# Two graph-attention layers on one Trainium2 core: edge weights in three operations, another order of the stages, one pool for the large arrays

## The chip, the cores and the metric

The kernel runs on one core of one Trainium2 chip. The core has TensorE (PE) for matrix products, VectorE (DVE), ScalarE (ACT) and GpSimd (POOL) for the rest, and SyncE (SP), which here issues most of the DMA transfers. Each engine takes its instructions in the order in which the program wrote them, and waits for the others by semaphores. The metric is the device time of one execution in microseconds, as the median of several runs. Lower is better.

## The reference

The input is a batch of 32 graphs of 512 nodes with 512 features (x, float32) and their adjacency (32 x 512 x 512 integers). Two layers follow, each on a normalised and rectified copy of x, and each added to x:

```python
h = jnp.maximum(_layernorm(x, axis=-1), 0.0)
x = x + _L0_gnn_ref(h, adj, ...)      # one head, no projection
h = jnp.maximum(_layernorm(x, axis=-1), 0.0)
x = x + _L1_gnn_ref(adj, h, ...)      # 512 -> 4 heads of 256, ELU, then 1024 -> 512 with one head
```

All three attentions (layer 0, and the two inside layer 1) have the same form. Every node has two scores, a and c, which are dot products of its features with two vectors. The weight between two nodes is the softmax of a leaky ReLU (slope 0.2) of a + c, taken over the neighbours only:

```python
e = jax.nn.leaky_relu(asrc[:, :, None, :] + adst[:, None, :, :], NEG_SLOPE)
e = jnp.where(mask[..., None], e, NEG_INF)
attn = jax.nn.softmax(e, axis=1)
out = jnp.einsum('bsdh,bshf->bdhf', attn, xl)
```

## The kernel before

**Tiles.** The 512 nodes of a graph are T = 4 blocks of 128 partitions (P). A matrix of weights E is a tile of 128 x 4 x 512 float32: block t of the rows, all 512 columns. A graph has six of them: one for layer 0, four for the heads of layer 1's first attention, one for its second.

**Stages of a graph.** `layer0_scores` (normalise, rectify, two dot products a block on DVE, the masks, the edge weights), `layer0_out` (E times h, added to x), `layer1_in` (normalise, rectify, transpose h on PE, spill x to DRAM), `layer1_project` (the product with W1, by a scheme of seven products of half-size blocks in place of eight, `products`), `layer1_scores` and `layer1_head` for each of four heads, `layer2_project`, `load_back` (x from DRAM) and `layer2_out`. The product with W also gives the scores a and c, as two more columns. All products are float32; PE shows two records for each. The attention products are at L688 (`aggregate`), those with W at L904 (`product`).

**The edge weights** (`edge_weights`, L638 to 679). The score a is made a row (512 values, the same on all partitions) in a PSUM bank. DVE adds the mask to it and takes the maximum (L647, four times), so that every column n has the largest neighbouring a; from that and c comes the guard m, the largest exponent of each column (L653, L655). The guard is made a row, too. Then each of the four blocks takes four operations: ACT computes the leaky ReLU of row c plus column a (Prelu, L669), DVE subtracts the guard's row (L672), POOL adds the mask, which is 0 or a large negative number (L675), and ACT takes the exponential (L678). The division by the sum comes after the product, by a column of ones that stands beside the values (L700, L974).

**Two ways to make a row of a column.** `spread` (L585) transposes the column, broadcast to 128 x 128, on PE: four transposes (L510) into one PSUM bank. `in_lines` (L603) transposes the narrow columns once (L609), copies them out of PSUM, and writes them to a small DRAM array, `lines` (L615); `row_of` (L620) reads a line back to all 128 partitions (L625), into one of three buffers `row`; `in_bank` (L632) copies such a row to PSUM by ACT (L635). The scores of layer 1's heads go through `lines`. The guards of layer 0 and of the second attention go through `lines` as well, except in the first and the last graph. The guards of layer 1's four heads go through `spread`, by the last argument of the call in `layer1_scores`, `edge_weights(ac(0), ac, lines, 2 * j, m1T, m1, True)`.

**Masks.** POOL's queue loads the adjacency of a graph (L729) twice, for layer 0 and for layer 1, and SP issues its transpose (L739).

**The order of the work.** The kernel records each operation with its engine, an assumed cost, its dependences and the buffers that it takes, and a planner (`Plan`) orders them all before anything is emitted. It runs through time: whichever engine is free next takes the ready operation with the lowest rank. A buffer is taken when the first operation that needs it is placed and is free after the last; kinds named in `in_turn` are handed out in the order of the program. The rank is the position in the program, less a share of the operation's `ahead` (400 for rows and first constants, -300 for what is needed later). Six shares are tried, each with a second draft ranked by the latest start that the first draft allows (`latest`), and the draft with the earliest end is emitted. The loop over graphs b (L1091 on) has this order: masks and projection of b; read-back and output of b-1; load of x(b+2); the four heads of b, each with its weights one head ahead; layer 0's output and layer 1's input of b+1; layer 0's scores of b+2; second projection and weights of b.

**Buffers.** x 2, masks 5 in four kinds, h 1, hT 1, pair 3, xl2 1, E 5, row 3, spill 2, eight PSUM banks (acc).

## Time and profile before

| | |
|---|---|
| median of 3 runs | 3626.27 us |
| fastest and slowest run | 3624.45 and 3626.67 us |
| profiled execution, its own time as the profile gives it (its span) | 3621.9 us |
| busy: PE, DVE, ACT, POOL | 3537.2, 2814.5, 2214.8, 1500.5 us |
| moved by DMA | 378.82 MB |
| row reads from `lines` | 442 of 256 KB, 3.3 us from issue to landing |

The profiled execution has no time but the span, from its first to its last instruction; the median of the runs is 4.4 us more. How to read the lines: in the table of engines stand the busy microseconds, the share of the span and the number of instructions. The slices cut the span in 40 and give busy tenths. The chain that ended last goes back from the last instruction to what released it, and so on; its shares say which engine and which line the end hangs on. A row of a timeline has start, duration, engine, line, operation, output and inputs, and in brackets the idle time before it and what ended that. Durations of PE overlap, so the cost of one of its instructions is the distance of two starts.

### The profile page before, as it was taken

The page shows a single profiled execution, that of the slowest core. Times are in us where ns is not written, and L with a number is a line of the kernel's source. Part 1 is how long each engine was busy: PE and PEld are TensorE (multiplying, and loading weights), DVE is VectorE, ACT ScalarE, POOL GpSimd, SP SyncE. Part 2 cuts the span into 40 slices and gives each one's busy share as a digit, 9 for nine tenths or more (in the row PEclk, how much of TensorE's full clock was granted, in tenths as well). Part 3 has the DMA queues.
Part 4 walks back from the last instruction along what each step waited for, and adds up shares of the span by engine and source line. Part 5 has one row for each costly group of instructions (what it writes and reads, how often), then busy time and mean ns, then how long its engine had stood idle before and what let it go on. Part 6 is the DMA issues. An engine that isn't in the chain of part 4 may idle for free.

```text
span 3621.9 us, 50432 instructions
## 1 busy us (share of the span) xinstructions
PE 3537.2 (98%) x16852; PEld 3039.8 (84%) x16852; DVE 2814.5 (78%) x7468; ACT 2214.8 (61%) x3801; POOL 1500.5 (41%) x1306
## 2 busy tenths in 40 slices
PE   4899999999999999999999999999999999999998
PEld 3788888888888888888888888888888888888887
DVE  7978778777778787778787788777787877787755
ACT  2665566665666665666655666655666656666554
POOL 4534335443344343344344354443443433453432
PEclk9999999999999999999999999999999999999999
DMA  6254333444334443334443334443344433344321
GB/s 171 56 126 116 91 97 107 105 123 105 99 96 111 110 120 97 100 104 102 122 114 96 98 107 101 124 113 91 99 112 105 120 98 100 104 105 117 103 75 43
DMA packets 510375, 378.82 MB, mean 105 GB/s; under 512 B 348345, under 2 KB 386977, under 8 KB 510113
## 3 DMA queue, kind: packets, MB, share of 16 engines
q1 hardware_dynamic: 476320, 342.03, 33.0%
q0 software_dynamic: 33792, 33.56, 6.5%
q8 instruction: 132, 2.16, 0.2%
q14 instruction: 131, 1.07, 0.1%
HBM read 257.16 MB, written 68.01 MB: 90 GB/s over the span
## 4 chain that ended last, share of the span: by engine, by line
PE 88%; DVE 2%; DMA 1%; issue 0%; POOL 0%; ACT 0%; DVEq 0%; SPq 0%; ACTq 0%
PE acc L688 44%; PE acc L904 39%; PE acc L510 4%; DVE junk L647 1%; PE acc L609 1%; DVE E L672 0%; POOL E L675 0%; DMA lines<-row 0%; DMA row<-lines 0%; DVE x L706 0%; DVE v L977 0%; ACT acc L635 0%; ACT E L669 0%; DVE col L655 0%; DVE col L653 0%
## 5 line engine op out<-in xcount | busy, mean ns | idle before, releaser
L675 POOL TENSOR_TENSOR E<-E,m 128x512 f32<-128x512 f32 x640 | 759.4, 1215 | 545.8 <-DVE E L672 413.7
L688 PE MATMUL acc<-pair,E 128*128 128x257 f32 (+1 forms) x4160 | 935.0, 380 | 5.9 <-ACT E L678 3.9
L688 PEld LDWEIGHTS acc<-pair,E 128*128 128x128 f32 x4160 | 783.0, 189 | 122.0 <-ACT E L678 4.7
L678 ACT ACTIVATE E<-E 128x512 f32<-128x512 f32 x768 | 472.9, 623 | 218.1 <-POOL E L675 217.1
L904 PE MATMUL acc<-w_T,E 128*128 128x257 f32 (+1 forms) x2048 | 515.7, 380 | 0.2 <-POOL w_T L492 0.2
L669 ACT ACTIVATE E<-row,ac 128x512 f32<-128x512 f32 x760 | 507.5, 710 | 3.2 <-DMA row<-lines 3.0
L672 DVE TENSOR_TENSOR E<-E,acc 128x512 f32<-128x512 f32 x768 | 491.7, 675 | 19.0 <-ACT acc L635 11.7
L688 PE MATMUL acc<-h,E 128*128 128x257 f32 (+1 forms) x2048 | 487.0, 382 | 16.3 <-ACT E L678 16.3
L688 PE MATMUL acc<-xl,E 128*128 128x257 f32 x1984 | 448.9, 380 | 2.7 <-ACT E L678 2.7
L647 DVE CUSTOM_DVE_ANT_0 junk<-m1T,acc 128x512 bf16<-128x512 bf16 x640 | 436.0, 681 | 15.0 <-PE acc L510 3.4
L688 PEld LDWEIGHTS acc<-h,E 128*128 128x128 f32 x2048 | 385.0, 191 | 70.8 <-ACT E L678 17.5
L904 PEld LDWEIGHTS acc<-w_T,E 128*128 128x128 f32 x2048 | 385.3, 190 | 56.3 <-POOL w_T L492 0.6
L688 PEld LDWEIGHTS acc<-xl,E 128*128 128x128 f32 x1984 | 371.2, 190 | 53.3 <-ACT E L678 2.9
L917 DVE TENSOR_TENSOR pair<-acc,pair 128x258 f32<-128x258 f32 (+1 forms) x390 | 165.0, 424 | 320.3 <-PE acc L904 258.5
L543 ACT COPY pair<-acc 128x258 f32<-128x258 f32 (+1 forms) x400 | 147.6, 370 | 297.3 <-PE acc L904 293.5
L729 POOL DMA_DIRECT2D m<-in_adj_dram x64 | 51.6, 806 | 590.9 <-DVE col L647 540.7
L533 ACT ACTIVATE h<-x,col,col 128x512 f32<-128x512 f32 x256 | 187.6, 804 | 176.4 <-issue 108.8
L675 POOL TENSOR_TENSOR E<-E,m0T 128x512 f32<-128x512 f32 x128 | 144.7, 1155 | 353.5 <-DVE E L672 353.5
L543 ACT COPY xl<-acc 128x257 f32<-128x257 f32 x190 | 68.8, 369 | 331.3 <-PE acc L904 331.3
L904 PE MATMUL acc<-w,hT 128*128 128x258 f32 x1024 | 269.6, 383 | 0.0
L904 PE MATMUL acc<-w,E 128*128 128x257 f32 (+1 forms) x1024 | 267.7, 381 | 0.0
L977 DVE SCALAR_TENSOR_TENSOR v<-acc,r,b_r 128x256 f32<-128x256 f32 x512 | 244.5, 478 | 9.2
(108 smaller groups left out, 5524.3 us busy)
## 6 DMA issues: line engine op xcount, KB each, us to landing
row<-lines SPq DMA_DIRECT2D x442, 256.0 KB, 3.3
x<-in_x_dram SPq DMA_DIRECT2D x32, 1024.0 KB, 13.6
m<-in_adj_dram POOLq DMA_DIRECT2D x64, 512.0 KB, 5.7
spill<-x SPq DMA_DIRECT2D x32, 1024.0 KB, 4.4
x<-spill SPq DMA_DIRECT2D x32, 1024.0 KB
out_dram<-x SPq DMA_DIRECT2D x30, 1024.0 KB, 4.2
v<-row SPq DMA_TRANSPOSE x192, 2.7
out_dram<-x SPq DMA_DIRECT2D x8, 256.0 KB, 2.0
```

The source lines that it names most:

```text
L510: op("PE", on_pe(P, transpose=True), lambda: nc.tensor.transpose(dst_of(), src_of(), identity), src, dst(part), ahead)
L533: lambda: nc.scalar.activation(h.at[:, t, :D], X.at[:, t, :], AF.Relu, bias=nmr.at[:, t : t + 1], scale=rstd.at[:, t : t + 1]),
L543: nc.scalar.copy(dst_of(), src_of())
L647: lambda t=t: nc.vector.tensor_tensor_reduce(by_blocks(junk), mask_row(mask_max, t), by_blocks(a_row.at), 1.0, LOWEST, ALU.add, ALU.max, a ...
L669: lambda t=t: nc.scalar.activation(E.at[:, t, :], c_row.at, AF.Prelu, bias=a_of(t), scale=1.0, alpha=SLOPE),
L672: op("DVE", on_dve(N), lambda t=t: nc.vector.tensor_sub(E.at[:, t, :], E.at[:, t, :], m_row.at), m_row(*ROW) + E(t), E(t))
L675: lambda t=t: nc.gpsimd.tensor_add(by_blocks(E.at[:, t, :]), by_blocks(E.at[:, t, :]), mask_row(mask, t)),
L678: op("ACT", on_act(N), lambda t=t: nc.scalar.activation(E.at[:, t, :], E.at[:, t, :], AF.Exp), E(t), E(t))
L688: lambda s=s: nc.tensor.matmul(acc.at[:, :n], E.at[:, s, node_block(t)], of(s), start=(s == 0), stop=(s == T - 1)),
L904: lambda k=k: nc.tensor.matmul(acc.at[:, :width], at[a]()[:, k, node_block(r)], weight_of(w, k, c), start=(first and k == 0), stop=(k == n ...
L917: op("DVE", on_dve(width), lambda: nc.vector.tensor_add(place(), acc.at[:, :width], place()), acc(0) + token, token)
L977: lambda i=i, v=v, acc=acc, r=r: nc.vector.scalar_tensor_tensor(v.at[:, i, :], acc.at[:, :F], r.at, b1_r[:, h * F : (h + 1) * F], op0=ALU. ...
```

## The change

- **Edge weights.** Since leaky(a + c) is a + 0.2 c + max(0.8 c, -0.8 a), and 0.2 c is the same for a whole column of the softmax, the weights are computed as exp(a + max(0.8 c, -0.8 a) + mask - g), where g is the guard less 0.2 c. The vectors that give c are scaled by 0.8 once (`scaled`). A block takes three operations: POOL subtracts g's row from the mask, DVE takes the maximum of row c (in PSUM) and a column and adds POOL's result, ACT takes the exponential with column a as bias.
- **Guards.** They have a function of their own (`guards`), for both heads of a pair at once. All go through `lines`, but for the first graph's layer 0 and the last graph's second attention. The rows of g and c are read into the last two blocks of the tile E itself.
- **Order.** `layer2_project` of b-1 comes after the projection of b; two heads' weights come first, then layer 0's output and layer 1's input of b+1, the load of x(b+2), the heads, layer 0's scores, and the read-back and output of b-1 last.
- **Leads.** The position in the program is replaced by the PE work ahead of the operation, less a lead for its stage (`LEADS`, a table in microseconds; a star stands for PE's operations, "first" and "last" for the first and last graphs). One draft is made.
- **Pools.** h, hT, pair, xl2 and E share eleven places (`big`), handed out in any order; the masks share five in turn; `row` has two places, spill four.

```diff
-    AHEAD, DRAFTS = (0.25, 0.5, 0.75, 1.0, 1.25, 1.5), 1
+    LEADS = {
+        "first LXsoon": -3, "first Csoon": -892.2, "first C": -652.8, "first Clater": -1055, "first S0": -896.9,
+        "first S0M0": -82.9, "first S0g": 0, "first S0g*": 1.5, "first S0e*": -109.4, "first S0e": -112.3,
+        "first O0*": -186.7, "first O0": -606.7, "first I1": 109.2, "first I1*": 57.3, "first LX": -57.3,
+        "first S0*": 51.5, "M1": -176.1, "P1": 226.4, "P1*": -47.2, "S1": -178.5, "S1*": 2390.8, "S1g": 0.2,
+        "S1g*": 11.1, "S1e": -430.4, "O0*": -17, "O0": -41.5, "I1": 243.9, "I1*": 1.2, "LX": 103.4, "H*": -14.8,
+        "H": 677, "S0": -969.2, "S0M0": 0.1, "S0*": -7.8, "S0g": 0, "S0g*": 2.2, "S0e": -22, "P2": 297.1, "P2*": 3.6,
+        "P2g": 183, "P2g*": 72.1, "P2e": -385.7, "LB": 167.8, "O2*": -83.3, "O2": -311.4, "last M1": 12.4,
+        "last P1": -359.3, "last P1*": 175.2, "last P2": -440.7, "last P2*": 163.9, "last P2g": 201.5,
+        "last P2g*": 165.4, "last P2e": -174.1, "last S1": -53.8, "last S1*": 674.7, "last S1g": -338.7,
+        "last S1g*": 107.8, "last S1e": 93.3, "last H*": 160.8, "last H": -242.6, "last LB": -4, "last P2e*": 130.2,
+        "last O2*": -97.7, "last O2": -248.8,
+    }
...
+        rank, work, best = [], 0.0, None
+        for engines, cost, _, _, _, lead, _ in self.ops:
+            rank.append(work - 1e3 * self.LEADS[lead])
+            if engines[0] == "PE":
+                work += cost[0][0]
...
-        "m0": places("m0", 1, [P, T, N], BF16),
-        "m0T": places("m0T", 1, [P, T, N], BF16),
-        "m1": places("m1", 2, [P, T, N], BF16),
-        "m1T": places("m1T", 1, [P, T, N], BF16),
-        "h": places("h", 1, [P, T, D + 1]),
-        "hT": places("hT", 1, [P, KD, N]),
-        "pair": places("pair", 3, [P, T * 2 * XL]),
-        "xl2": places("xl2", 1, [P, T, 2 + D + 1]),
-        "E": places("E", 5, [P, T, N]),
+        "m": places("m", 5, [P, T, N], BF16),
+        "big": places("big", 11, [P, T * 2 * XL]),
...
-    plan = Plan(slots, ("x", "spill", "m0", "m0T", "m1", "m1T", "h", "hT", "pair", "xl2", "v"))
+    plan = Plan(slots, ("x", "spill", "v", "m"))
...
+        scaled(lambda: ws_r, D, W["w0"](0), W["w0"]("src"), SOON)
+        scaled(lambda: b0_r, 1, W["w0"](2), W["w0"]("rest"), SOON)
+        scaled(lambda: flat(att[0])[:, HF : 2 * HF], HF, att[0](1), att[0](1), LATER)
...
+    @plan.part("g")
+    def guards(scores, ac, lines, n, mask_max, near):
+        op(
+            "DVE", on_dve(n * T), lambda: nc.vector.tensor_scalar(ac.at[:, 4 : 4 + n, :], ac.at[:, 0 : 2 * n : 2, :], SLOPE - 1.0, None, op0=ALU.mult),
+            scores, ac("negated"),
+        )
+        g = Buffer("guard")
+        for j in range(n):
+            a_of = lambda t, j=j: ac.at[:, 2 * j, t : t + 1]
+            a_row = spread(scores, a_of) if near & 1 else in_bank(row_of(lines, 2 * j))
...
+        if near & 2:
+            return g, None
+        return g, in_lines(lambda: g.at[:, :n, :].rearrange("p n t -> p (n t)"), g(*range(n)), n)
...
+    @plan.part("e")
+    def edge_weights(scores, ac, lines, j, guard, mask):
+        g, guard_lines = guard
+        E = Buffer("big", as_rows)
+        c_at, g_at = (lambda: E.at[:, T - 2, :]), (lambda: E.at[:, T - 1, :])
+        if guard_lines is None:
+            bank = spread(g(j) + E("place"), lambda t: g.at[:, j, t : t + 1])
+            op("ACT", on_act(N), lambda: nc.scalar.copy(g_at(), bank.at), bank(*ROW), E(T - 1))
+        else:
+            row_of(guard_lines, j, g_at, E(T - 1))
+        c_of = lambda t: ac.at[:, 2 * j + 1, t : t + 1]
+        c_row = spread(scores + E("place"), c_of) if lines is None else in_bank(row_of(lines, 2 * j + 1, c_at, E(T - 2)))
         for t in range(T):
             op(
+                "POOL", on_pool(N, True),
+                lambda t=t: nc.gpsimd.tensor_sub(by_blocks(E.at[:, t, :]), mask_row(mask, t), by_blocks(g_at())),
+                E(T - 1) + mask(*ROW), E(t), lock=True,
+            )
+            op(
+                "DVE", on_dve(N, 1.0, True),
+                lambda t=t: nc.vector.scalar_tensor_tensor(
+                    E.at[:, t, :], c_row.at, ac.at[:, 4 + j, t : t + 1], E.at[:, t, :], op0=ALU.max, op1=ALU.add
                 ),
+                c_row(*ROW) + E(t) + ac("negated"), E(t),
+            )
...
-            op("DVE", on_dve(N), lambda t=t: nc.vector.tensor_sub(E.at[:, t, :], E.at[:, t, :], m_row.at), m_row(*ROW) + E(t), E(t))
...
-            op("ACT", on_act(N), lambda t=t: nc.scalar.activation(E.at[:, t, :], E.at[:, t, :], AF.Exp), E(t), E(t))
...
+                lambda t=t: nc.scalar.activation(E.at[:, t, :], E.at[:, t, :], AF.Exp, bias=ac.at[:, 2 * j, t : t + 1]),
...
+        plan.stage = "last " if b == B - 1 else ""
         masks1(b)
         layer1_project(b)
         if b:
-            load_back(b - 1)
-            layer2_out(b - 1, ROW if b < B - 1 else ROW[:EARLY], b < B - 1)
-        if b + 2 < B:
-            load_x(b + 2)
-        Es = []
-        for h in range(H):
-            Es.append(layer1_scores(b, h))
-            if h:
-                layer1_head(b, h - 1, Es[h - 1])
-        layer1_head(b, H - 1, Es[H - 1])
+            layer2_project(b - 1)
+        Es = [layer1_scores(b, 0), layer1_scores(b, 1)]
         if b + 1 < B:
             layer0_out(b + 1)
             layer1_in(b + 1)
         if b + 2 < B:
+            load_x(b + 2)
+        for h in range(H):
+            if h + 2 < H:
+                Es.append(layer1_scores(b, h + 2))
+            layer1_head(b, h, Es[h])
+        if b + 2 < B:
             layer0_scores(b + 2)
-        layer2_project(b)
-
+        if b:
+            load_back(b - 1)
+            layer2_out(b - 1, ROW if b < B - 1 else ROW[:EARLY], b < B - 1)
+    layer2_project(B - 1)
     layer2_out(B - 2, ROW[EARLY:], False)
     load_back(B - 1)
     layer2_out(B - 1, ROW, False)
```

## The prediction

> **What bounds the kernel now.** I read the engine table and the slices first, to see which engine is full and where it is not, then the chain that ended last, then PE's waits by stage, and last PE's own timeline in one graph, to price what the change takes from it.
>
> ```profile
> span 3621.9 us, 50432 instructions
> PE 3537.2 (98%) x16852; PEld 3039.8 (84%) x16852; DVE 2814.5 (78%) x7468; ACT 2214.8 (61%) x3801; POOL 1500.5 (41%) x1306
> PE   4899999999999999999999999999999999999998
> ...
> PE 88%; DVE 2%; DMA 1%; issue 0%; POOL 0%; ACT 0%; DVEq 0%; SPq 0%; ACTq 0%
> PE acc L688 44%; PE acc L904 39%; PE acc L510 4%; DVE junk L647 1%; PE acc L609 1%; DVE E L672 0%; POOL E L675 0%; DMA lines<-row 0%; DMA row<-lines 0%; DVE x L706 0%; DVE v L977 0%; ACT acc L635 0%; ACT E L669 0%; DVE col L655 0%; DVE col L653 0%
> ```
>
> PE is full and carries the chain; nothing else has over 2%. L688 are the attention products, L904 the projections, L510 the transposes in sets. The stages (columns: length; busy us and instructions by engine; granted clock; DMA share; GB/s) say where PE still stands:
>
> ```profile
> 0.00:100.00 100.00, 47.05 (x185) 37.85 (x186) 75.77 (x230) 24.75 (x46) 40.56 (x40) 0.93 0.60 157
> 100.00:200.00 100.00, 87.31 (x397) 71.55 (x397) 84.07 (x219) 58.33 (x96) 46.04 (x40) 0.97 0.27 76
> 400.00:1000.00 600.00, 599.78 (x2872) 516.92 (x2871) 468.86 (x1246) 373.46 (x652) 246.84 (x218) 1.00 0.42 108
> 3500.00:3622.00 122.00, 106.58 (x474) 89.28 (x473) 69.05 (x170) 59.60 (x102) 34.25 (x29) 0.92 0.18 55
> ```
>
> From 400 to 3500 us PE stands still for 1.8 us in all (3100 less the four stages' 599.78, 999.83, 998.70, 499.92). There only PE's own work counts. All else it loses is at the two ends: 53 us in the first 100, 13 in the next, 15 in the last 122.
>
> **PE's work: the guards' transposes.** Before, every head of layer 1 turns its guard column into a row with four transposes on PE (`spread`, called with near true). After, one transpose for two heads, a write to DRAM and two broadcast reads do it. 32 graphs x 4 heads = 128 sets of four go, 64 single ones come: 448 PE instructions fewer of 16852. A window of PE's timeline inside one graph (start, duration, line):
>
> ```profile
> 1005.44 0.65 PE L510 MATMUL acc<-ident,col 128*128 128x128 f32 x4
> 1005.92 3.63 PE L688 MATMUL acc<-xl,E 128*128 128x257 f32 x16
> ...
> 1014.78 0.65 PE L510 MATMUL acc<-ident,col 128*128 128x128 f32 x4
> 1015.27 8.84 PE L688 MATMUL acc<-pair,E 128*128 128x257 f32 x40
> ...
> 1023.95 0.60 PE L510 MATMUL acc<-ident,col 128*128 128x128 f32 x4
> 1024.38 1.89 PE L688 MATMUL acc<-h,E 128*128 128x257 f32 x8
> ...
> 1084.55 0.27 PE L609 MATMUL acc<-ident,col 128*4 128x128 f32 x1
> 1084.66 0.60 PE L904 MATMUL acc<-w,E 128*128 128x258 f32 x2
> ```
>
> The durations overlap, so I count from start to start: a set costs 0.48, 0.49 and 0.43 us, mean 0.467; a single one 0.11. 128 x 0.467 - 64 x 0.11 = 59.7 - 7.0 = **52.7 us less** (48.0 at 0.43, 55.7 at 0.49). All matmuls stay: 240 a graph, two records each. Since PE is covered by nothing in those 3100 us, this comes off the end in full if the rest keeps up.
>
> **The edge weights: three operations a tile in place of four.** Gone: ACT's Prelu (760 + 8, 512 us busy) and DVE's subtraction (768 x 675). New: POOL subtracts the guard row from the mask (same shapes as the addition that it replaces, 1155 to 1215 ns), DVE does max and add with the score row in PSUM, ACT does Exp with a bias column (taken as the Prelu with its column, 512 us in place of 473). The DVE form is not in the trace at 512 columns. Bounds: 675, as the subtraction that reads PSUM; 834, as L998's two-tensor form at 512 in SBUF. L977 and L706, the same instruction with PSUM at 256, take 477; adding 256 columns at (675 - 424) / 254 = 0.99 ns (L672 against L917) gives 730, which I take: +42 us on DVE in all. The sum for DVE, with 128 small multiplications of a score column (L802's kind, 224 ns: 29), is 2885 us, 81% of the new span. ACT: -512, +39 for the bias, +111 for 190 score rows copied to PSUM (585 each), -36 for 62 guard rows no longer copied, +16 for 64 evictions (254): 1833 us. None of this is on the path in the long stage: PE hides it, and by 20 us a graph (DVE 86 of 109.7 us). If that cover were gone, DVE's +0.07 us would count on each tile.
>
> **The guards' rows.** 128 more row reads (338 ns of SP issue each: 43 us) and 64 more line writes (304 ns: 19 us), 33.5 MB more on 378.8; the DMA engines are 42% busy. The latency of a guard grows from 1.1 us (four transposes) to transpose 0.3, eviction 0.25, write 1.8, read 3.3: 5.7 us, and the read now lands in the tile E itself, so that SP waits for a free place and all rows, mask transposes and spills behind it wait too. The nearest row is the identical round trip of the scores, already there 64 times in layer 1: it is inside the 1.8 us of waits. Bounds: 0, as those; upwards 2.7 to 2.8 us (PE's wait for Exp in the first and last graphs) on each of 64 pairs, 175 us. I take 5 us, since the near row says almost nothing.
>
> The Trainium skill's "DMA: Bandwidth & Descriptors", section "Latency and other measured facts", speaks against this part: about 2 us of fixed cost for every DMA, most of it the round trip to HBM. Two trips would be 4 us by it, against the 5.1 us of this trace; by either the guard is late unless the order has it 4 to 6 us early.
>
> **Order and pools.** The second layer's projection of graph b moves behind the first layer's of b+1 (56 products, 24 us at 0.434); its output moves to the end of that turn; two heads' weights come ahead of the next graph's output of layer 0. Moved with them: the line writes and row reads and the read-back of x on SP (now behind the load of graph b+2), and the masks' loads on POOL, which already waits 591 us in all ahead of them. Five mask places are still five, eleven large ones still eleven (1+1+3+1+5), only handed out freely. On average this costs nothing: the cover is PE's backlog; without it a late x is 13.6 us, once a graph. The leads replace six trial orders by one order; a lead says how far ahead or behind its place in PE's work an operation ranks.
>
> **Start.** Now PE's first product waits until 44.10 us: SP issues the transposed mask only at 30.54, behind the weights, POOL starts on it at 42.06, although the guards are there at 29.96. After, by the leads, SP takes x(0), x(1), ten transfers of layer 1's vectors and weights, and only then ws_r. Now those eight weight loads are issued until 14.8; so ws_r would be issued at about 16 and land (its row: 5.7) at 22, against dots that now start at 11.42. Then 6.0 us of dots, 0.7 of transposes, 3.0 of maxima, 0.3, four transposes 1.1, a copy 0.6, POOL 1.2, DVE 0.7, ACT 0.7: 36 to 38 us. The mask's transpose ranks ahead of the last nine loads: issued at 20 to 26, plus the present 11.5, 32 to 38. I take the start at 40: **-4**. Bounds: -13 (the mask issued as soon as it is made, at 19) and +10 (dots delayed in full on top of the present order).
>
> **End.** Now the last graph's edge weights stand uncovered:
>
> ```profile
> 3597.19 1.11 PE L510 MATMUL acc<-ident,col 128*128 128x128 f32 x4 [3.01 <-DVE col L655]
> 3601.05 16.99 PE L688 MATMUL acc<-pair,E 128*128 128x257 f32 x64 [2.74 <-ACT E L678]
> ```
>
> From PE's last projection (it would end about 3592.1) to 3601.05 are 9 us, of which 1.1 is transposes, and the last 64 products take 17.0 us where 64 x 0.217 is 13.9. After, output of graph 30 (64 records, 14 us) ranks behind the last projection (leads -97.7 against +163.9) and can stand in that gap. Filled, 8 + 3 = 11 us go; unfilled, the new chain is 0.6 us longer (a copy). I take **-7**. The granted clock is 0.92 in this stage.
>
> The skill's "TensorE: Matmul & The Clock Gate", section "What's actually happening", says that an idle window of 3.4 us halves the clock until one busy window has passed; that loses 1.7 us, an estimate, where the row loses 3.1. By it the end would give 9.8 in place of 11.
>
> **Sum.** -52.7 + 5 - 4 - 7 = -58.7 us. The profiled execution's span is 3621.9, which would become 3563.2; the median of the runs, 3626.27, lies 4.4 us above it, and I carry that over: **3567.6, say 3568**. A measurement of this kernel tells about 0.2%, 7 us.
>
> **Rivals.** (1) The start gains in full as well: 12 in place of 4 there, 11 at the end, no new stalls: 3626.3 - 52.7 - 23 = 3551. For it: separate leads for the first and last graphs. Against: ws_r so late in SP's queue. (2) The gain is partly given back: heads wait for guards on a third of the 64 pairs by 1 to 1.5 us (some 20 to 32 us), no gain at the ends: 3626 - 53 + 26, about 3599. For it: margins are thin now (one tile of weights finishes at 1032.5 and the 32 records of a head start at 1035.2); against: 1.8 us of waits. (3) Slower: SP holds the guard's row back. Now six transposes of v, which wait for ACT, stretch over 20.35 us of SP's queue from 1019.94; a row read behind them is up to 20 us late, and every later row behind a read that waits for E's place. It decides from 64 pairs x 0.92 us = 59 us; at 2 us a pair the time is 3626 - 59 + 128 = 3695. Against: the rows of the scores stand in the same queue now and cost nothing. (4) The planner's new order does not do what it says and PE's idle grows as much as its work falls: 3626.
>
> **How the numbers follow.** Forecast (3556 to 3582): 0.53. Rival 1 (3540 to 3556): 0.16. Rival 2 (3582 to 3619): 0.15. Rival 4 (within 7 us): 0.04. Rival 3: 0.12. Faster 0.84, same 0.04, slower 0.12. Outside 3543 to 3620 lie rivals 3 and 4 and a fifth of rival 1, some 0.19. The cost of DVE's new form at its ends (-42, +80 us from the one taken, off the path) moves none of it while PE covers it.
>
> **What would show it.** PE with 448 fewer instructions and L510's sets for col gone but for the first and last graphs; PE's waits from 400 to 3450 us under 10 us; ACT near 1830, DVE near 2890; the first product near 40 us; no wait of 8 us ahead of the last 64 products. Wrong it is if PE waits for Exp or for a guard's eviction once in every graph.

## The result, and the profile after

| | before | after |
|---|---|---|
| median of the runs | 3624.79 us | 3635.08 us |
| fastest and slowest run | 3623.02 and 3626.67 | 3627.05 and 3642.64 |
| span of the profiled execution | 3621.9 us | 3636.5 us |

The ratio is 1.0025, with an interval of 1.0019 to 1.0032: a little slower, where 1.6% faster was forecast. The page of the kernel after: its span, its table of engines, PE's slices, and the chain that ended last, by engine and by line:

```profile
span 3636.5 us, 49863 instructions
PE 3487.2 (96%) x16404; PEld 2998.4 (82%) x16404; DVE 2834.7 (78%) x7596; ACT 1891.2 (52%) x3204; POOL 1500.9 (41%) x1394
PE   3999999999999999999999999999999999999999
...
PE 76%; DVE 10%; DMA 9%; issue 2%; POOL 1%; ACT 0%; SPq 0%; POOLq 0%; DVEq 0%
PE acc L988 37%; PE acc L760 36%; DMA m<-in_adj_dram 8%; DVE junk L698 3%; PE acc L553 2%; DVE big L741 2%; PE acc L652 1%; DMA big<-lines 1%; DVE x L778 1%; DVE col L705 1%; DVE guard L710 1%; DVE st L559 1%; POOL big L736 1%; DVE v L1086 1%; DVE m L855 1%
```

PE has the 448 instructions fewer and 50.0 us less work. But the chain no longer stays on PE: 88% have become 76%, and a load of the adjacency (`m<-in_adj_dram`), which isn't among the lines of the chain before, holds 8%. In the new numbering the attention products are L760, the projections L988, the transposes L553, a single narrow transpose L652. The table by stage (length; busy us and instructions of PE, PEld, DVE, ACT, POOL; clock; DMA share; GB/s):

```profile
0.00:100.00 100.00, 39.34 (x149) 30.76 (x150) 77.96 (x227) 20.81 (x32) 39.93 (x40) 0.91 0.66 168
100.00:400.00 300.00, 291.79 (x1368) 247.99 (x1367) 257.49 (x705) 175.37 (x298) 135.74 (x122) 0.99 0.42 106
400.00:3500.00 3100.00, 3025.91 (x14280) 2607.70 (x14279) 2416.92 (x6476) 1639.18 (x2789) 1283.33 (x1197) 1.00 0.44 114
3500.00:3637.00 137.00, 130.15 (x613) 111.96 (x611) 82.31 (x189) 55.80 (x86) 41.91 (x35) 1.00 0.23 68
```

A stage's length less PE's busy time is PE's idle time. The whole difference of the two profiled executions comes out of it:

| | before | after | difference |
|---|---|---|---|
| PE busy | 3537.2 | 3487.2 | -50.0 |
| PE idle, 0 to 400 us | 67.6 | 68.9 | +1.2 |
| PE idle, 400 to 3500 us | 1.8 | 74.1 | **+72.3** |
| PE idle, from 3500 us to the end of the span | 15.3 | 6.4 | -9.0 |
| sum, the span | 3621.9 | 3636.5 | +14.6 |

So the gain was made, and given back in the steady graphs. PE's waits of the kernel after in that stretch (total us, times, longest us) are two, each once in a graph:

```profile
PE acc L760 <- DVE v L1065: 45.3, 27, 3.9
PE acc L652 <- DVE guard L710: 28.7, 27, 2.1
```

DVE itself waits in the same stretch for the adjacency:

```profile
DVE m L855 <- DMA m<-in_adj_dram: 56.1, 27, 4.3
```

**The first wait: the mask.** `v L1065` is an eviction on DVE that takes half a microsecond and depends on nothing new. A timeline of one graph (start, duration, engine, line, operation, in brackets the idle time before it and what ended that; SPq is SP issuing a transfer) shows what stands ahead of it:

```profile
1013.36 0.37 SPq L922 DMA_DIRECT2D spill<-x  x1
1014.36 0.37 SPq L791 DMA_DIRECT2D x<-in_x_dram  x1
1018.48 0.36 SPq L931 DMA_DIRECT2D x<-spill  x1
1018.70 0.82 POOL L802 DMA_DIRECT2D m<-in_adj_dram  x1 [0.30 <-DVE r L1062]
...
1030.13 0.69 DVE L855 TENSOR_SCALAR m<-m 128x2048 bf16<-128x2048 bf16 x1 [2.95 <-DMA m<-in_adj_dram]
1032.20 0.48 DVE L1065 SCALAR_TENSOR_TENSOR v<-acc,r,b_r 128x256 f32<-128x256 f32 x1
...
1032.73 3.08 PE L760 MATMUL acc<-big,big 128*128 128x257 f32 x8 [2.54 <-DVE v L1065]
```

POOL issues the adjacency's load 0.2 us after SP has issued the third of three 1 MB transfers. It lands 11.4 us later. DVE has the first operation on the mask (L855) as its next instruction, stands 2.95 us for it, and the eviction that would free a PSUM bank waits behind it. Then PE stands. The kernel before had the same four transfers, but far apart:

```profile
996.48 0.79 POOL L729 DMA_DIRECT2D m<-in_adj_dram  x1 [0.30 <-POOL E L675]
...
1005.30 0.68 DVE L777 TENSOR_SCALAR m<-m 128x2048 bf16<-128x2048 bf16 x1
...
1014.49 0.39 SPq L718 DMA_DIRECT2D x<-in_x_dram  x1
...
1059.71 0.36 SPq L840 DMA_DIRECT2D spill<-x  x1
...
1063.94 0.36 SPq L848 DMA_DIRECT2D x<-spill  x1
```

There the adjacency landed after 5.7 us, and the same mask operation (then L777, at 1005.30, 9 us after the load's issue) never waited. A graph loads its adjacency twice, and only layer 1's load, the one shown, is late now: over the 27 steady graphs it lands after 10.4 us (median; 9.5 to 12.7) in place of 5.7, while layer 0's lands after 5.5. (The page's medians over all 64 loads, 5.7 and 6.9, mix the two.) The new order of the stages brought the four transfers together.

**The second wait: a guard.** It is the guard of the second attention, which went through `lines` before the change too. PE's narrow transpose stands 0.79 us for it in this graph:

```profile
984.73 18.13 POOL L736 TENSOR_TENSOR big<-m,big 128x512 f32<-128x512 bf16 x16 [19.55 <-DMA big<-lines]
...
1000.88 0.76 DVE L705 TENSOR_TENSOR col<-ac,col 128x4 f32<-128x4 f32 x1
...
1001.96 0.92 DVE L710 SCALAR_TENSOR_TENSOR guard<-col,col 128x4 f32<-128x4 f32 x1
...
1003.02 0.27 PE L652 MATMUL acc<-ident,guard 128*4 128x128 f32 x1 [0.79 <-DVE guard L710]
```

Two operations on 128 x 4 elements take 0.76 and 0.92 us, while POOL works through sixteen subtractions of the edge weights in a row. When POOL is idle they take 0.16. Counted over 400 to 3400 us, for single operations of DVE (mean us, number), by whether POOL was at work on arrays at their start (POOL's issue of a transfer is counted as idle):

| kernel, line, operation | reads | POOL at work | POOL idle |
|---|---|---|---|
| before, L525, `col<-mv,col` 128x4 | two tensors in SBUF | 1.227 (28) | 0.163 (27) |
| before, L653, `col<-ac,col` 128x4 | two in SBUF | 0.513 (27) | 0.149 (137) |
| before, L655, `col<-col` 128x4 | two in SBUF (the same twice) | (0) | 0.148 (164) |
| after, L705, `col<-ac,col` 128x4 | two in SBUF | 0.982 (54) | 0.158 (108) |
| after, L710, `guard<-col,col` 128x4 | two in SBUF | 0.910 (27) | 0.154 (135) |
| after, L560, `mv<-st` 128x2 | one in SBUF | 0.176 (86) | 0.172 (130) |
| after, L687, `ac<-ac` 128x4 and 128x8, times a constant | one in SBUF | 0.951 (33) | 0.167 (75) |
| after, L741, `big<-acc,ac,big` 128x512 | one in PSUM, one in SBUF | 0.739 (486) | 0.736 (162) |

The kernel before has the same effect, as two of its rows show (POOL at work until 802.85):

```profile
797.68 5.17 POOL L675 TENSOR_TENSOR E<-E,m 128x512 f32<-128x512 f32 x4 [5.57 <-DVE E L672]
...
800.97 0.72 DVE L653 TENSOR_TENSOR col<-ac,col 128x4 f32<-128x4 f32 x1
```

But its guard operations met POOL 27 times, and L655 never; in the kernel after the two that replace them meet it 81 times.

### The profile page after: what moved, and what is told of

Same layout as the page of the kernel before. It is cut to its first block, busy times and chain, and to the rows that moved or that the text cites. A ratio compares the mean times of both kernels' runs of the same rounds, so it can differ in the third digit from the quotient of the medians.

```text
span 3636.5 us, 49863 instructions
## 1 busy us (share of the span) xinstructions
PE 3487.2 (96%) x16404; PEld 2998.4 (82%) x16404; DVE 2834.7 (78%) x7596; ACT 1891.2 (52%) x3204; POOL 1500.9 (41%) x1394
## 4 chain that ended last, share of the span: by engine, by line
PE 76%; DVE 10%; DMA 9%; issue 2%; POOL 1%; ACT 0%; SPq 0%; POOLq 0%; DVEq 0%
PE acc L988 37%; PE acc L760 36%; DMA m<-in_adj_dram 8%; DVE junk L698 3%; PE acc L553 2%; DVE big L741 2%; PE acc L652 1%; DMA big<-lines 1%; DVE x L778 1%; DVE col L705 1%; DVE guard L710 1%; DVE st L559 1%; POOL big L736 1%; DVE v L1086 1%; DVE m L855 1%
## 5 line engine op out<-in xcount | busy, mean ns | idle before, releaser
L760 PE MATMUL acc<-big,big 128*128 128x257 f32 (+1 forms) x8192 | 1876.2, 381 | 61.7 <-DVE v L1065 47.8
L760 PEld LDWEIGHTS acc<-big,big 128*128 128x128 f32 x8192 | 1540.8, 190 | 307.1 <-DVE v L1065 59.9
L736 POOL TENSOR_TENSOR big<-m,big 128x512 f32<-128x512 bf16 x768 | 889.6, 1186 | 667.6 <-DMA big<-lines 455.9
L988 PE MATMUL acc<-w_T,big 128*128 128x258 f32 (+1 forms) x3072 | 776.4, 382 | 1.6 <-DVE big L968 1.6
L988 PE MATMUL acc<-w,big 128*128 128x258 f32 (+1 forms) x3072 | 769.2, 381 | 0.9 <-POOL big L969 0.6
L748 ACT ACTIVATE big<-big,ac 128x512 f32<-128x512 f32 x768 | 539.9, 719 | 265.6 <-DVE big L741 258.0
L988 PEld LDWEIGHTS acc<-w_T,big 128*128 128x128 f32 x3072 | 582.4, 191 | 91.3 <-DVE big L968 2.0
L988 PEld LDWEIGHTS acc<-w,big 128*128 128x128 f32 x3072 | 572.1, 190 | 87.1 <-ACT big L586 1.0
L741 DVE SCALAR_TENSOR_TENSOR big<-acc,ac,big 128x512 f32<-128x512 f32 x768 | 555.6, 738 | 23.7 <-POOL big L736 20.7
L698 DVE CUSTOM_DVE_ANT_0 junk<-m,acc 128x512 bf16<-128x512 bf16 x768 | 525.1, 684 | 18.5 <-DVE ac L687 0.4
L988 PE MATMUL acc<-w_-T,big 128*128 128x258 f32 (+1 forms) x1024 | 254.3, 380 | 1.9 <-DVE big L1001 1.9
L1065 DVE SCALAR_TENSOR_TENSOR v<-acc,r,b_r 128x256 f32<-128x256 f32 x512 | 246.0, 481 | 7.4
L988 PEld LDWEIGHTS acc<-w_-T,big 128*128 128x128 f32 x1024 | 191.5, 189 | 33.7 <-DVE big L1001 3.4
L576 ACT ACTIVATE big<-x,col,col 128x512 f32<-128x512 f32 x256 | 195.7, 804 | 23.2 <-DVE col L568 20.4
```

The lines of the kernel that those rows point to most:

```text
L698: lambda t=t, amax=amax, a_row=a_row: nc.vector.tensor_tensor_reduce(by_blocks(junk), mask_row(mask_max, t), by_blocks(a_row.at), 1.0, LOW ...
L736: lambda t=t: nc.gpsimd.tensor_sub(by_blocks(E.at[:, t, :]), mask_row(mask, t), by_blocks(g_at())),
L741: lambda t=t: nc.vector.scalar_tensor_tensor(E.at[:, t, :], c_row.at, ac.at[:, 4 + j, t : t + 1], E.at[:, t, :], op0=ALU.max, op1=ALU.add),
L748: lambda t=t: nc.scalar.activation(E.at[:, t, :], E.at[:, t, :], AF.Exp, bias=ac.at[:, 2 * j, t : t + 1]),
L760: lambda s=s: nc.tensor.matmul(acc.at[:, :n], E.at[:, s, node_block(t)], of(s), start=(s == 0), stop=(s == T - 1)),
L988: lambda k=k: nc.tensor.matmul(acc.at[:, :width], at[a]()[:, k, node_block(r)], weight_of(w, k, c), start=(first and k == 0), stop=(k == n ...
```

## The experiments

Two theories for the standing time were to be told apart from each other and from the prediction's own rivals. (A) The adjacency is late because of the transfers beside it, and DVE, which works in order, passes the delay to PE. (B) The second attention's guard is late because POOL holds back DVE's small operations. The rivals: the rows of layer 1's guards through DRAM cost the time after all; or DVE is simply behind, so that each wait that is removed comes back elsewhere. In the diffs, `plan.shift` holds one operation back, with what depends on it, in the emitted order, behind the given number of operations of its own engine; the rest of the order stays.

**1. The mask's operations later.**

```diff
-        load_adj(b, m1)
+        load_adj(b, m1); plan.shift += [(len(plan.ops) + n, 12) for n in range(1 + T) if b > 2]
```

> The changed kernel with one thing moved: from the fourth graph on, DVE's five operations that make layer 1's mask out of the loaded adjacency stand some twelve DVE operations later; all other orders are the same. Theory: DVE waits there for an adjacency transfer that lands later than the planner assumed (56 us from 400 to 3500 us), and through it PE waits for the eviction behind (45 us, and a lower clock after each wait). Then PE's waits for v go and the time falls from 3635 by 45 to 65 us, to 3570 to 3590. Rival: PE has run out of prepared weights and waits at the next late step instead; then the time stays above 3620.

Measured: 3591.4 us (3589.5 to 3593.7), a ratio of 0.991 (0.9895 to 0.9924) to the kernel before. The wait for v is gone from the steady graphs; one of 13.7 us (27 times) for layer 0's scores has come, and the guard's is still there with 24.8. Most of theory A's gain appears, 1.4 us short of the expected range.

**2. The guard's transpose later.** The second attention's transpose of its guard stands six products later on PE.

```diff
-        if near & 2:
-            return g, None
+        if near & 2: return g, None
+        plan.shift += [(len(plan.ops), 6)] if plan.stage == "P2g" else []
```

> The changed kernel with one thing moved: PE's single transpose of the second attention's guard stands six products (2.6 us) later, with what hangs on it. Theory: PE waits about 1 us a graph (28.7 us from 400 to 3500) because DVE's two small operations for the guard take 0.8 and 0.9 us in place of 0.15 while POOL works beside them. Then this wait goes: 3635 - 29 = 3606, 3598 to 3612. Rival: the wait for v grows by what is gained here, or POOL's weights come late by 2.6 us a graph; then 3630 or more.

Measured: 3639.5 us (3636.7 to 3644.9), ratio 1.0044 (1.0029 to 1.0059): no gain. PE's waits:

```profile
PE acc L760 <- DVE v L1065: 49.0, 27, 4.1
PE acc L553 <- ACT big L576: 7.4, 28, 0.3
PE acc L760 <- DVE x L778: 6.2, 13, 1.1
```

The guard's wait is gone, but 17 of its 28.7 us stand at the other three now, and the time shows nothing of the rest. While DVE loses 2.2 us a graph to the mask (60.0 us in 27 waits of L855 in this run), a later transpose hides little. The expected time was missed.

**3. Both.**

> Both moves at once. Theory: all steady waits of PE go, 74 us of standing and 5 to 20 us of lowered clock: 3541 to 3561, about 3553, which is the sum that was forecast without the stalls. Rival (the pools or the longer guard chain are short in themselves): other waits come in, above 3600.

Measured: 3588.7 us (3586.2 to 3589.5), ratio 0.9901 (0.9884 to 0.9917). Not the sum: 2.7 us better than the mask's operations alone, far above the expected 3541 to 3561, and below the rival's 3600 too. 11.2 us for layer 0's scores, 6.7 for an ACT operation and 5.5 for the eviction of x remain: some of what is held back is missed elsewhere.

**4. The kernel before, with layer 1's guards through DRAM.** Of the change, only this part.

```diff
-        return edge_weights(ac(0), ac, lines, 2 * j, m1T, m1, True)
+        return edge_weights(ac(0), ac, lines, 2 * j, m1T, m1, False)
```

> The kernel before with the one change that takes work from PE: the guards of layer 1's heads go through DRAM (the last argument of the call false), one head at a time, the planner ordering anew. 128 sets of four transposes go, 128 single ones come: 59.7 - 14.1 = 45.6 us less on PE. Theory (the rows through DRAM are not what stalls): 3625 - 46 = 3579, 3570 to 3600. Rival (the guards' round trip through DRAM makes heads wait): 3615 or more.

Measured: 3953.6 us (3946.1 to 3957.5), ratio 1.0906 (1.089 to 1.0922), 375 us over what was expected. The largest of PE's waits:

```profile
PE acc L510 <- ACT h L533: 61.9, 26, 4.0
PE acc L904 <- POOL E L886: 59.8, 33, 3.5
PE acc L904 <- ACT pair L578: 24.8, 13, 1.9
```

So this part of the change can't be taken alone: with the old ranks, the old order and the separate pools it costs more than it saves. In the kernel after, where the leads, the order, the common pool and guards made for two heads at once come with it, no steady wait is left that names the new rows. Which of these makes them free was not tried apart.

**5. A small spill.** The order of the kernel after, but the spill of x and its read-back move the first of four blocks only, 0.25 MB in place of 1 MB each; the other blocks are left out, so the output is not the reference's.

```diff
-... nc.sync.dma_start(away.at.rearrange("(t p) f -> p t f", p=P), xb.at),
+... nc.sync.dma_start(away.at.rearrange("(t p) f -> p t f", p=P)[:, :1], xb.at[:, :1]),
...
-... nc.sync.dma_start(xb.at, away.at.rearrange("(t p) f -> p t f", p=P)),
+... nc.sync.dma_start(xb.at[:, :1], away.at.rearrange("(t p) f -> p t f", p=P)[:, :1]),
```

> The changed kernel, every order the same, but x is spilled and read back only for the first of its four blocks (three quarters of 2 MB a graph are left out, so the result is not the reference's). Theory: the adjacency lands 11.4 us after its issue because the spill, the read-back and the load of x run beside it. Then it lands in 7 to 9 us, DVE's wait for it (56 us from 400 to 3500 us) falls under 15, PE's wait for v (45) with it, and the time is 3580 to 3605, near that of the run in which the mask was made later (3591). Rival: POOL's own transfer is slow because VectorE keeps POOL from writing its descriptors; then landing and time stay, 3625 to 3642.

Measured: 3571.0 us (3570.3 to 3571.8), ratio 0.985 (0.9836 to 0.9865), 9 us below the expected range. No instruction has another place. Layer 1's adjacency lands after 7.6 us (median of 27) in place of 10.4; without a wait DVE comes to it 8.4 us after its issue, and DVE's wait for it is gone. Of PE's waits only the guard's is left:

```profile
PE acc L652 <- DVE guard L710: 28.1, 28, 1.6
PE acc L760 <- DVE v L1065: 0.4, 1, 0.4
```

So the bytes beside the adjacency make it late. The 64 us (3635.1 less 3571.0) are more than the wait's 45: PE busy is 3467.6 us for the same 16404 instructions, 19.6 less, at a mean granted clock of 0.997 in place of 0.994 (more on it at the end). The clock accounts for some 11 of the 19.6, by an estimate from these means (0.006 x 3636.5 less 0.003 x 3569.2); where the rest comes from the runs don't show.

**6. More operations later.** Run 1, with the second attention's transpose three products later and that of layer 0's scores five.

> As the run with both moves, with the guard's transpose of the second attention moved by three products in place of six, and the transpose of layer 0's scores by five, from the fourth graph on. Theory: what is left of PE's steady waits are these two places (11.2 us for the scores, 12 us of side effects of the six), so 3588.7 - 10 to 20 = 3569 to 3579. Rival: taking away one wait brings the next one, since the order has no slack anywhere; then 3584 to 3592.

Measured: 3580.5 us (3578.1 to 3583.9), ratio 0.9877 (0.9862 to 0.9892), just outside the expected range.

**7. The start.** Run 6, with layer 0's vectors (`ws_r` and two more) moved up in SP's queue, right behind the first x.

```diff
-        self.ops, self.stage = [], ""
+        self.ops, self.stage, self.shift, self.soon = [], "", [], [1, 2, 3]
...
+    for i in reversed(plan.soon):
+        order.remove(i)
+        order.insert(1 + order.index(0), i)
```

> As the run before, and at the start SP issues the two score vectors and the bias of layer 0 right behind the first x, ahead of layer 1's weights; all other orders are the same. Theory: the dot products of the first graph, which begin at 28.2 us, begin 4 to 6 us earlier and so does PE's first product (47.8): 4 to 6 us less than the run before. Rival: the start hangs on the transposed mask or on VectorE's other work; then within 2 us of it.

Measured: 3580.4 us (3578.6 to 3583), ratio 0.9878 (0.9862 to 0.9895), as run 6. The dots of graph 0 begin earlier, at 25.6 us, but the first product still stands until 48.3: the late vectors were not what held it. By the trace POOL's weight sum (until 45.6) and DVE's dots of graph 1 stand between; which of the two decides was not tried.

**8. Layer 1's guards by PE again.** The kernel after, with only this part undone; the order is planned anew, with a lead of 11.1 for the new stage (107.8 in the last graph).

```diff
-            AC[b] = (ac, lines, guards(ac(0), ac, lines, 2, m1T, 0))
+            AC[b] = (ac, lines, guards(ac(0), ac, lines, 2, m1T, 2))
```

> The changed kernel with one part undone: the guards of layer 1's heads are made rows by four transposes on PE again (and copied into the tile by ACT); the planner orders anew, the new stage's lead taken as 11.1 (107.8 in the last graph). Theory (448 instructions are worth 50 us, and PE is the bound in either form): PE busy 3530 to 3545, time 3635 + 50 or more, 3670 to 3720. Rival (the round trip through DRAM is what costs the stalls): the stalls go, 3635 or less.

Measured: 3677.4 us (two runs), ratio 1.0144 (1.0123 to 1.0164). PE is busy for 3540.3 us with 16852 instructions, 53.1 over the kernel after: undoing the part gives the prediction's 52.7 back. The new plan also happens to issue the read-back of x 2.6 us behind the adjacency's load; that lands after 6.3 us (median of 27), and 1.8 us of the wait for v are left. With that, and with other waits that come in (12.0 us for L576), the time grows by 42 us and not by 53.

**9. The read-back three places later.** If the bytes beside the adjacency are at fault, moving one of the three transfers should do, with nothing left out.

```diff
-        X[b], away = Buffer("x"), S.pop(b)
+        X[b], away = Buffer("x"), S.pop(b); plan.shift += [(len(plan.ops), 3)] if 2 < b < B - 2 else []
```

> The changed kernel's own order, but in the steady graphs SP issues the 1 MB read-back of x three of its operations later, behind the v transposes, so that the adjacency of the next graph shares the DMA engines with one large transfer less when it starts. Theory (the adjacency is late because three 1 MB transfers run beside it): it lands 8 to 9 us after its issue where it took 11.4, the wait of the products for the eviction of v falls from 45 us to under 15, the wait for the second attention's guard stays at 25 to 30, and the time is 3580 to 3605. Rival (the spill and the load of x alone keep it late): that wait stays above 30 and the time above 3620.

Measured: 3577.5 us (3574.6 to 3582.3), ratio **0.9872** (0.9858 to 0.9885): 57.6 us less than the kernel after, and 2.5 below the expected range. The timeline of one graph:

```profile
1001.71 0.37 SPq L922 DMA_DIRECT2D spill<-x  x1
...
1007.06 0.82 POOL L802 DMA_DIRECT2D m<-in_adj_dram  x1 [0.30 <-DVE r L1062]
...
1016.08 0.69 DVE L855 TENSOR_SCALAR m<-m 128x2048 bf16<-128x2048 bf16 x1 [0.56 <-DMA m<-in_adj_dram]
...
1025.43 0.53 SPq L931 DMA_DIRECT2D x<-spill  x1
```

The read-back is issued at 1025.43, 18 us behind the adjacency's load instead of 0.2 us ahead of it. The adjacency is there after 9.0 us in place of 11.4, and DVE stands 0.56 us in place of 2.95. Over the 27 steady graphs the median is 7.4 us (6.4 to 10.7) in place of 10.4. PE's waits, which were 45.3 and 28.7 us, and DVE's, which was 56.1:

```profile
PE acc L652 <- DVE guard L710: 26.2, 27, 1.6
PE acc L760 <- DVE v L1065: 4.9, 6, 1.2
DVE m L855 <- DMA m<-in_adj_dram: 8.1, 7, 2.2
```

That is theory A. The order of all engines but SP, and so DVE's part in it, is that of the kernel after.

**10 and 11. Together.** Run 10 is run 9 with the mask's operations and the transpose of layer 0's scores later, as above; run 11 has the second attention's transpose three products later besides.

> The later read-back, the five mask operations twelve DVE operations later, and the transpose of layer 0's scores five products later; the second attention's guard stays where it was. Theory (the mask's lateness and the layer-0 scores' wait go together, and the guard's 28 us are left alone): waits of 25 to 30 for the guard, under 5 for all others, 3560 to 3578. Rival (DVE's lag moves the wait to another eviction, as it did when the mask operations alone were moved): 3578 to 3592.

> As the run before, with the transpose of the second attention's guard row three products later. If a guard's wait can be hidden once DVE is no longer late for anything else: 10 to 20 us under the run before, 3545 to 3570. Rival (the wait moves to the next row or eviction): within 5 us of the run before.

Measured: run 10 3575.5 us (3571.7 to 3578.3), ratio 0.9864 (0.9851 to 0.9878); run 11 **3570.8 us** (3566.6 to 3575.1), ratio **0.9851** (0.9837 to 0.9864), 1.5% under the kernel before and the fastest that computes everything. PE's largest waits in run 11:

```profile
PE acc L553 <- ACT big L576: 7.1, 27, 0.3
PE acc L760 <- DVE x L778: 6.3, 12, 0.9
PE acc L760 <- DVE big L741: 3.9, 2, 2.9
```

The guard's 27.6 us of run 10 have become 1.4, but 13 of them are now at two other places. Run 11 gains 4.7 us on run 10, and the ranges of the two overlap, so the rival of its expectation, within 5 us, held: hiding DVE's delay behind more products pays back at most a small part of its 27.6 us.

**12. POOL's subtractions cut short.** Run 5 once more, and after the first 24 of the 192 tiles of weights (from the fifth graph's heads on) POOL subtracts the guard's row in one of four blocks of columns. Three quarters of these sums are left out, so the output is not the reference's.

```diff
-... nc.gpsimd.tensor_sub(by_blocks(E.at[:, t, :]), mask_row(mask, t), by_blocks(g_at())),
+... nc.gpsimd.tensor_sub(by_blocks(E.at[:, t, :])[:, :w], mask_row(mask, t)[:, :w], by_blocks(g_at())[:, :w]),
```

> The kernel with the small spill and read-back (one of four blocks), in which from the seventh graph on POOL subtracts the guard in one of the four blocks of columns alone; every instruction stays in its place, three quarters of POOL's sums are left out, so the result isn't the reference's. Theory (DVE's small operations on the guard are held back while POOL works on the same memory): POOL's subtractions take about 0.3 us where they took 1.1, the two guard operations of DVE fall from 0.76 and 0.92 us to 0.15 to 0.3, the wait for the second attention's guard falls from 28 us to under 8, and the time to 3535 to 3555 from 3571. Rival (the guard is late for another reason, DVE's place in its own order): the wait stays above 20 and the time above 3560.

Measured: 3540.3 us (3538.9 to 3541.4), ratio 0.9768 (0.9754 to 0.9781), 30.7 us less than run 5. PE's waits, and the two groups of DVE's small operations (busy us, mean ns), in the steady graphs:

```profile
PE acc L652 <- DVE guard L710: 1.7, 2, 1.4
PE acc L992 <- DVE big L972: 0.9, 1, 0.9
```

```profile
L705 DVE TENSOR_TENSOR col<-ac,col 128x4 f32<-128x4 f32 x167 | 27.7, 166 | 0.0
L710 DVE SCALAR_TENSOR_TENSOR guard<-col,col 128x4 f32<-128x4 f32 x167 | 26.4, 158 | 0.0
```

The same two groups in the kernel after:

```profile
L705 DVE TENSOR_TENSOR col<-ac,col 128x4 f32<-128x4 f32 x162 | 70.1, 433 | 0.0
L710 DVE SCALAR_TENSOR_TENSOR guard<-col,col 128x4 f32<-128x4 f32 x162 | 45.3, 280 | 0.0
```

No instruction has moved, DVE's operations are as short as with an idle POOL, and the guard's wait is gone. That is theory B. (A short subtraction took 0.45 us, not 0.3 as expected.) The 30.7 us are a little more than the wait's 28.1; POOL's weights are also ready sooner in this run. The adjacency took 9.2 us again (median), but POOL, free sooner, issues it 11.3 us ahead of its use. With both causes away PE stands for 3.0 us from 400 to 3500 us, where it stood 1.8 in the kernel before and 74.1 after.

## Why the prediction was wrong

It forecast 3568 us, with 3543 to 3620 as its range; 3635 came. By its own steps:

- **PE's work, -52.7.** Right: -50.0 between the two kernels, whose mean granted clocks are nearly the same (0.995 and 0.994), and 53.1 when the part is undone (run 8). Without the waits for the mask the clock is 0.997 (run 9), and the same 16404 instructions keep PE busy for 3470.8 us, 16.4 less than in the kernel after.
- **The edge weights.** DVE's form at 512 columns was taken as 730 ns and takes 738. ACT was forecast at 1833 us and is 1891, DVE at 2885 and is 2835. That they stay off the path holds; but POOL's half of this part is what holds back DVE's guard operations (run 12), which the prediction didn't weigh.
- **The guards' rows, +5 (bounds 0 to 175).** The new rows of layer 1 cost PE nothing in the steady graphs: there is no wait for Exp, and none for a pair's guard. So the rival with SP holding the rows back fell as well. What waits once a graph is the guard of the second attention, 28.7 us. The prediction had named such a wait as its sign of being wrong, but looked for its cause in the latency of the trip through DRAM; it lies before the trip, in DVE's two operations. The row that would have shown it was in the trace of before: L525 and L653 take 1.23 and 0.51 us beside POOL in place of 0.16 and 0.15. The prediction priced the round trip by transpose, eviction, write and read, and not the two operations ahead of them.
- **Order and pools, 0.** This is the step that failed: "On average this costs nothing: the cover is PE's backlog; without it a late x is 13.6 us, once a graph." It counted the moved transfers on SP's and POOL's queues, and asked whether each would itself be late. No wait of PE names x's load. The adjacency was late, because the others had come beside it: 5.7 us became 10.4 (11.4 in the graph shown), while DVE, where nothing makes it wait, comes to it after 8.4 (run 5). The cover named, PE's backlog, is no cover for a DVE that stands at the mask with PE's evictions behind it. Price: 45.3 us of standing, and in time, with the lowered clock, 58 us (run 9) to 64 (run 5).
- **Start, -4 (bounds -13 to +10).** The wrong sign, inside its bounds: the first product starts at 47.78 us in place of 44.10 (forecast: 40); from 0 to 400 us PE stands 1.2 us longer in all. The dots begin at 28.2 us, not 22: `ws_r` is issued at 15.66, as forecast, but `wd_r` only at 23.35, behind a mask's transpose. Delaying `ws_r` was rightly seen as a delay, but run 7 shows that it isn't the one that counts.
- **End, -7.** Right as to the gap, and too small in all: -9.0 of idle time in the table, and no wait of 8 us ahead of the last 64 products. Besides, the granted clock from 3500 us on is 1.00 in place of 0.92, some 8.5 us by an estimate (0.08 x 106.6 us of PE's busy time there before); these are part of the -50.0, which the lower clock of the steady graphs offsets. (The prediction's side estimate for the end, 8 + 1.7, is 9.7 and not 9.8.)
- **The rivals.** The one with a partial loss from guards (3599) put 20 to 32 us on the guards of layer 1's pairs, which cost nothing; that the second attention's guard cost 28.7 is luck in the number, at another place and by another cause. The fourth, "PE's idle grows as much as its work falls", at 4 in 100, is what happened in kind: idle time grew by 64.5 us and work fell by 50.0, so the time lies 9 us above its 3626, outside the 7 us that it gave itself.

The Trainium skill's page "SBUF — State Buffer", sections "Terms" and "Who interferes with whom", states that a DVE instruction with two inputs in SBUF contends with a GpSimd instruction that reads SBUF, that the loser waits for the other's whole instruction, and that a DVE instruction with one such input contends only in a mode that uses both of DVE's ports, which a tensor with a scalar (as L687) can enter. The table of DVE's operations agrees: with two inputs 0.5 to 1.2 us in place of 0.15 to 0.16, 0.95 in place of 0.17 for L687, no change for L560, and none for the new form of 512 columns, which has one of its tensors in PSUM. The mean delays, 0.4 to 1.1 us, are at most the length of one subtraction, which takes 1.13 us here (18.13 us for sixteen).

## What to carry to other kernels

When stages are reordered, list for one period which large transfers are now issued within a few microseconds of each other, and add their lengths: a transfer that nobody moved can become the late one, and the engine that waits for it in order passes the delay on to all that stands behind. Then move one transfer, not the work that waits: one read-back three places later was worth 57.6 us, and moving the waiting operations or PE's transposes gave less or nothing. And look in the old trace at how long a small operation of DVE on two tensors takes while POOL is at work, before one of them is placed beside a long run of POOL's.

## What the runs showed of the hardware

- Beside three transfers of 1 MB, a 512 KB load of the adjacency took 10.4 us from issue to landing (median of the 27 steady graphs); with one of them moved away 7.4 (run 9), with two of them cut to a quarter 7.6 (run 5); 5.7 in the kernel before. The mean DMA busy share was 0.44 in the stretch: the average said nothing about it.
- DVE's operations on two tensors of 128 x 4 elements took 0.91 to 0.98 us (means) in place of 0.16 while POOL was at work on arrays, which was enough for a wait of PE in every graph.
- A wait of 2.54 us was followed by a halved clock of PE: the eight records after it took 2.87 us from start to start and the next four 1.53, where run 9, after a wait of 0.54 us, shows 1.84 and 0.87. The row of the kernel after for that stretch, with the granted clock, 0.50, as its third number from the end:

```profile
1033.51:1036.90 3.39, 3.39 (x10) 2.65 (x9) 1.05 (x5) 2.75 (x4) 1.10 (x2) 0.50 0.40 77
```

  Six of the 27 waits for v, of 1.94 to 3.87 us, are followed by such a stretch, and others of up to 2.42 us are not; in runs 5 and 9 the steady graphs have none. The Trainium skill's page "TensorE: Matmul & The Clock Gate", section "What's actually happening", puts the limit at an idle window of about 3.4 us; here less standing did it.
